# Two attention layers on one core: the first output group ahead of the value transposes, norm chunks between evictions

## The chip, the cores and the metric

The kernel runs on one core of one Trainium2 chip. The metric is the device time of one execution in microseconds (us). The engines of the core are named as the profile names them: PE (TensorE matmuls; PEld its weight loads), DVE (VectorE), ACT (ScalarE), POOL (GpSimd) and SP (SyncE, which here only issues DMA transfers). All data is fp32.

## The reference, cut to what matters

Two layers of the same shape run over x of (4, 32, 32, 768): a group norm over 32 groups of channels of each image, attention with 12 heads of 64 and decomposed relative position biases, an output projection, and a residual.

```python
x = x + _L0_conv_ref(_gn(x), L0_conv_Wqkv, L0_conv_Wproj, ...)
x = x + _L1_conv_ref(_gn(x), L1_conv_qkv_w, L1_conv_qkv_b, ...)

qkv = x @ Wqkv                                  # in each layer; layer 1 with a bias
rel_h = einsum('bhwc,hkc->bhwk', r_q, Rh)       # and rel_w likewise
scores = scale * einsum('bqc,bkc->bqk', q, k) + (rel_h[..., :, None] + rel_w[..., None, :])
out = einsum('bqk,bkc->bqc', softmax(scores), v)
return out @ Wproj + bproj
```

The norm's mean and variance are over a whole image's 1024 positions and 24 channels. So the norm of a layer's image needs the whole output of the layer before for that image.

## The kernel before, in words

**Images, pairs, units.** There are eight images in order (layer 0 images 0 to 3, then layer 1 images 0 to 3). An image is kept as six chunks of 128 channels by 1024 positions (`xn`). Heads go two at a time: 6 pairs an image, 48 in all. A pair has 8 units (n = 0 to 7), each the scores of 128 query positions for both heads against all 1024 keys. The loop at L521 goes over the 384 units; everything is issued by hand in the order of the code (`manual_schedule`, L497), so each engine works its own instructions in that order.

**One step of the loop** (L521 to L573) issues, in this order: the biases of the unit after next on POOL (L303); the scores of the next unit on PE (L315), with, for each of the two heads, a pass on DVE that adds the bias and finds the maximum (L324), and an exponential on ACT (L328); at n = 7 the transposes of the next pair's values on PE (`vt`, L252) with their copy out of PSUM on ACT (L253); the read-back of transposed softmax quarters (`pt<-td`, L363); at some steps a stage of the next image's norm; the softmax transposition of this unit on DVE (`turn`, L352), followed on every second step by a store to DRAM (`td<-tb`, L355); the reciprocal (L335, DVE) and the division (L338, POOL) of the next unit; then a share of a list of projection work. After n = 6 and n = 2 come the weighings of values with two quarters of the softmax (`av`, L378, copied out by DVE at L383).

**The list of projection work.** `todo` holds groups; `shares` says how many chunk matmuls of it each step takes: 6, 6, 0, 6, 12, 6, 0, 12 for n = 0 to 7. For each pair it holds six groups of the next pair's q, k and v (`pj`, L222, six chunks each; copied out by ACT at L232 or L234 and added by DVE at L235), then four groups of the output projection (`o`, L442, three chunks each, evicted by DVE). So at n = 7 the share of 12 is four output groups, whenever there are any.

**The output projection** of an image is done in parts: part 0 (heads 0 to 5) in pairs 3 to 5 of that image, evicted at L451 with output bias and residual, and stored as a partial sum to DRAM (`part<-res`); part 1 (heads 6 to 11) in pairs 0 to 2 of the next image, evicted at L454 with the partial sum loaded again (`res<-part`), followed in layer 0 by `bn_stats` for the next norm (L149). For the last image there is no next one: its parts 1 (chunks 3 and 4) and 2 (chunk 5) fill the last pair and the tail behind the loop (L574 to L586), where sums are kept on the chip (`sum`) from part 1 on.

**PSUM.** Scores have a pool of their own (L76). All other PE results (`pj`, `tp`, `vt`, `av`, `o`) share the two buffers of L77: what comes next on PE needs the buffer of what came two before, emptied by DVE or ACT.

**The norm of the next image.** At pair 3 four stages are issued (L556): at n = 1 per-channel statistics go to DRAM, at n = 3 they come back by group, at n = 6 `groups` computes the mean and inverse deviation (a square root on ACT at L187, for which ACT exchanges its function table and, for the next exponential, exchanges it back; then a reciprocal on DVE at L188 and a store), at n = 7 the result is spread to channels. At pair 4 the chunks are normed in place on DVE (`apply`, L197): chunk 0 at n = 2, chunk 1 at n = 6, chunks 2 to 5 at n = 7 after the first output group.

**Transfers.** SP issues nearly all DMAs in program order, and an issue that waits holds up those behind it. Lists (`early`, `later`, `behind`, `behind2`) put issues off to the next steps.

Of the kernel before, what the change touches and what calls it, by code (L numbers as in the profile page):

```python
# [54 lines left out]
def attention_blocks(ctx: ExitStack, tc: tile.TileContext, a: dict, out: bass.AP):  # L55
    nc = tc.nc
# [27 lines left out]
    NI = len(images)  # L84
# [45 lines left out]
    bo = []  # L130
# [32 lines left out]
    def norm(im):  # L163

        per = dram2.tile([C, 2], FP, tag="per", name=f"per_{im}")
        back = dram2.tile([C, 2], FP, tag="back", name=f"back_{im}")  # L170
        g = small.tile([NG, 2, GS, 2], FP, tag="g", bufs=1, name=f"g_{im}")
        st = small.tile([NG, 2, 6], FP, tag="gst", bufs=1, name=f"gst_{im}")
        mv = small.tile([NG, 3, 2], FP, tag="gmv", bufs=1, name=f"gmv_{im}")
        nrm = small.tile([P, NC, 2], FP, tag="nrm", bufs=2, name=f"nrm_{im}")

        def gather():
            nc.sync.dma_start(out=per.rearrange("(c p) s -> p c s", p=P), in_=mv_of[im])

        def by_group():
            nc.sync.dma_start(out=g[:, 0, :, :], in_=per.rearrange("(g k) s -> g k s", k=GS))  # L180

        def groups():
            for k in range(2):
                nc.vector.bn_stats(st[:, k, :], g[:, 0, :, k])
                nc.vector.bn_aggr(mv[:, k, :], st[:, k, :])
            nc.vector.tensor_scalar(mv[:, 2, 0:1], mv[:, 0, 1:2], mv[:, 1, 0:1], EPS, ALU.add, ALU.add)
            nc.scalar.activation(mv[:, 2, 1:2], mv[:, 2, 0:1], AF.Sqrt)  # L187
            nc.vector.reciprocal(mv[:, 2, 0:1], mv[:, 2, 1:2])  # L188
            for k, x in enumerate((mv[:, 0, 0:1], mv[:, 2, 0:1])):
                nc.vector.tensor_copy(g[:, 1, :, k], x.to_broadcast([NG, GS]))  # L190
            nc.sync.dma_start(out=back.rearrange("(g k) s -> g k s", k=GS), in_=g[:, 1, :, :])

        def spread():
            nc.sync.dma_start(out=nrm, in_=back.rearrange("(c p) s -> p c s", p=P))

        def apply(c):
            nc.vector.tensor_scalar(  # L197
                xn_of[im][c], xn_of[im][c], nrm[:, c, 0:1], nrm[:, c, 1:2], ALU.subtract, ALU.mult
            )

        return [gather, by_group, groups, spread], apply


    qkv_of, v_of, rel_of, t_of = {}, {}, {}, {}
# [186 lines left out]
    def cuts(im):  # L391
        return [0, NC // 2, NC] if im + 1 < NI else [0, NC // 2, NC - 1, NC]

    parts = [(im, p, o, i) for im in range(NI) for p in range(2) for o in range(NC) for i in range(2)]
    place = {part: at for at, part in enumerate(parts)}
    part_of, res_of, sum_of = {}, {}, {}
    fetched = [0, 0]
# [1 line left out]
    def fetch(upto):  # L399

        while fetched[0] <= min(upto + 2, len(parts) - 1):
            im, p, o, i = parts[fetched[0]]
            c0, c1 = cuts(im)[p : p + 2]
            if i == 0:
                w = wopool.tile([P, NC // 2, P], FP, tag="wo", name=f"wo_{im}_{p}_{o}")
                nc.sync.dma_start(
                    out=w[:, : c1 - c0, :],
                    in_=a[f"wo{images[im][0]}"][o][:, c0 * P : c1 * P].rearrange(
                        "p (c o) -> p c o", o=P
                    ),  # L410
                )
                for c in range(c0, c1):
                    wo_of[im, o, c] = w[:, c - c0, :]
            fetched[0] += 1
        while fetched[1] <= min(upto, len(parts) - 1):
            im, p, o, i = parts[fetched[1]]
            l, b = images[im]
            if (p, o, i) == (0, 0, 0):
                part_of[im] = dram2.tile([C, S], FP, tag="part", name=f"part_{im}")
            res = iopool.tile([P, HALF], FP, tag="res", name=f"res_{im}_{p}_{o}_{i}")  # L420
            res_of[im, p, o, i] = res
            src = srcs[l][b] if p == 0 else part_of[im]
            nc.sync.dma_start(out=res, in_=src[o * P : (o + 1) * P, i * HALF : (i + 1) * HALF])
            fetched[1] += 1

    def fetch_last():
        im = NI - 1
        w = wpool.tile([P, NC, P], FP, tag="w", name="w_last")
        src = a[f"wo{images[im][0]}"].rearrange("o p (c k) -> c p o k", c=NC)
        nc.sync.dma_start(out=w, in_=src[NC - 1])  # L430
        for o in range(NC):
            wo_of[im, o, NC - 1] = w[:, o, :]
            sum_of[o] = xpool.tile([P, S], FP, tag="xn", name=f"sum_{o}")

    def project_out(im, p, o, i):
        l, b = images[im]
        rows = slice(o * P, (o + 1) * P)
        cols = slice(i * HALF, (i + 1) * HALF)
        c0, c1 = cuts(im)[p : p + 2]
        t = ps_m.tile([P, S], FP, tag="m", name=f"o_{im}_{p}_{o}_{i}")[:, :HALF]  # L440
        for c in range(c0, c1):
            nc.tensor.matmul(  # L442
                t, lhsT=wo_of[im, o, c], rhs=attn_of[im * NP + c][:, cols],
                start=(c == c0), stop=(c == c1 - 1),
            )
            if c < c1 - 1:
                yield True
        at_end = im + 1 == NI and p > 0
        res = sum_of[o][:, cols] if at_end else res_of[im, p, o, i]
        if p == 0:  # L450
            nc.vector.scalar_tensor_tensor(res, t, bo[l][:, o : o + 1], res, ALU.add, ALU.add)  # L451
        else:
            add = res_of[im, p, o, i] if p == 1 else res
            nc.vector.tensor_tensor(res, t, add, ALU.add)  # L454
        if p == 1 and l + 1 < LAYERS:
            stats(im + B, o, i, res)
        dst = part_of[im] if p == 0 else dsts[l][b]
        if at_end:
            if p == 2:
                nc.sync.dma_start(out=dst[rows, cols], in_=res)  # L460
        else:
            early.append(lambda: nc.sync.dma_start(out=dst[rows, cols], in_=res))
        if i == 1 and p < 2:
            (early if im + 1 == NI else later).append(lambda: fetch(place[im, p, o, i] + 4))
        yield True


# [5 lines left out]
    def run(todo):  # L473
        while todo:
            todo.pop(0)()
# [21 lines left out]
    with tc.manual_schedule(engines=ENGINES):  # L497
# [4 lines left out]
        for stage in stages:  # L502
            stage()
        for c in range(NC):
            apply(c)
        todo = prepare(0)
# [14 lines left out]
        for at, (g, n) in enumerate(units):  # L521
            im, pair = divmod(g, NP)
            end = im + 1 == NI
            if n == 0:
                shares = [6, 6, 0, 6, 12, 6, 0, 12]
                ins = (todo if at == 0 else []) + (prepare(g + 1) if g + 1 < NPAIR else [])
                if pair < 3:
                    if at == 0:
                        shares = [12, 6, 0, 6, 12, 6, 0, 0]
                    todo = ins + (put_out(im - 1, 1, range(4 * pair, 4 * pair + 4)) if im else [])  # L530
                elif pair < NP - 1:
                    todo = ins + put_out(im, 0, range(4 * pair - 12, 4 * pair - 8))
                    if pair == 3 and not end:
                        stages, apply = norm(im + 1)
                else:
                    todo = ins + put_out(im, 0, range(8, 12))
                    if end:
                        fetch_last()
                        todo += put_out(im, 1, range(12)) + put_out(im, 2, range(0, 12, 2))
                        shares = [0, 6, 6, 4, 2, 2, 0, 8]  # L540
            if pair < 3 and not end and n % 4 == 0 and 2 * pair + n // 4 < AHEAD:
                load_x(im + 1, 2 * pair + n // 4)
            if pair < 3 and im + 1 < B and n in (1, 3, 5, 6):
# [5 lines left out]
                biases(*units[at + 2])  # L549
            if at + 1 < len(units):  # L550
                scores(*units[at + 1])
            if late and n == NT - 1 or at == 1:
# [81 lines left out]
```

## Time and profile before

| | |
|---|---|
| time, median of 3 runs | 3668.21 us (3663.29 to 3672.43) |
| profiled execution | span 3666.7 us, mean granted PE clock 0.993 |
| busy share PE / DVE / POOL / ACT | 96% / 66% / 63% / 36% |
| L222 `pj`, L315 `s`, L378 `av`, L442 `o` on PE, busy | 1533.7, 751.1, 687.8, 524.0 us |
| DMA | 1090.58 MB, mean 297 GB/s |
| `td<-tb`, `pt<-td`: 1024 KB each, x384 each | median 5.8 and 7.7 us to landing |

The page's first part gives the busy time of each engine; the span less PE's busy time is what PE stood idle. The waits view says for which instruction an engine waited, in total and how often. The timeline gives start, length, engine, line, operation, `out<-in` and, in brackets, how long the engine had been idle and what ended it; matmuls of one kind are merged into one line (fp32 matmuls count twice, so a group of three chunks of L442 is six). The view of windows gives busy times and the granted PE clock of chosen stretches.

### The profile page before, as it was taken

The numbers are of one execution on the slowest core, as the hardware profiler recorded it, in microseconds if no ns is written. First come the engines' busy times: TensorE is split into PE (matmuls) and PEld (weight loads), VectorE is DVE, ScalarE is ACT, GpSimd is POOL, SyncE is SP. The second block draws the span as 40 slices with busy tenths as digits, with TensorE's granted clock in tenths as the row PEclk, the third lists the DMA queues.
The fourth block names the chain that finished last, engine by engine and source line by source line (L and its number), as shares of the span: only waits on it lengthen the run. The fifth ranks groups of instructions, "written<-read, shape, count | busy, mean of one in ns | idle before, by whom it ended". The sixth has DMA issues, their size and how long they took to land.

```text
span 3666.7 us, 51253 instructions
## 1 busy us (share of the span) xinstructions
PE 3530.5 (96%) x19200; PEld 1739.5 (47%) x19200; DVE 2401.9 (66%) x3533; ACT 1309.5 (36%) x1992; POOL 2298.0 (63%) x1548
## 2 busy tenths in 40 slices
PE   6999999999999999999999999999999999999998
PEld 3554444444445444444445444444445444444443
DVE  4676667766676676666666666666666667666664
ACT  2343333333333333333333333333333333333331
POOL 3776666665666666666666666666656666666662
PEclk9999999999999999999999999999999999999999
DMA  4998898888988888888898888988889888888877
GB/s 142 321 313 299 290 324 311 305 292 284 327 313 304 278 314 312 310 297 284 296 317 307 283 305 305 317 303 289 303 285 320 288 294 315 300 303 286 306 277 277
DMA packets 632345, 1090.58 MB, mean 297 GB/s; under 512 B 248096, under 2 KB 310304, under 8 KB 582944
## 3 DMA queue, kind: packets, MB, share of 16 engines
q1 hardware_dynamic: 581408, 1036.97, 80.8%
q10 hardware_dynamic: 50688, 50.34, 3.9%
q8 instruction: 151, 2.47, 0.3%
q14 instruction: 98, 0.80, 0.1%
HBM read 583.74 MB, written 503.41 MB: 296 GB/s over the span
## 4 chain that ended last, share of the span: by engine, by line
PE 88%; ACT 4%; DVE 3%; DMA 2%; issue 2%; SPq 0%; POOL 0%; DVEq 0%; ACTq 0%; POOLq 0%
PE pj L222 40%; PE s L315 18%; PE av L378 17%; PE o L442 10%; ACT sc L328 3%; PE tp L267 3%; DVE xn L197 1%; ACT v L253 1%; DVE sc L324 1%; DVE res L451 0%; DMA pt<-td 0%; DMA xs<-in_x 0%; DVE tb L352 0%; DMA w<-in_wqkv 0%; DMA part<-res 0%
## 5 line engine op out<-in xcount | busy, mean ns | idle before, releaser
L338 POOL TENSOR_SCALAR sc<-sc,sm 128x1024 f32<-128x1024 f32 x768 | 852.2, 1122 | 1265.8 <-DVE sm L335 1233.5
L222 PE MATMUL pj<-xn,w 64*128 64x512 f32 x6912 | 1533.7, 590 | 26.9 <-DVE xn L197 25.9
L303 POOL TENSOR_TENSOR sc<-rel 128x1024 f32<-128x1024 f32 x768 | 1457.0, 1918 | 42.1 <-DMA rel<-tdr 42.1
L328 ACT ACTIVATE sc<-sc,sm 128x1024 f32<-128x1024 f32 x768 | 879.1, 1145 | 1482.2 <-DVE sm L324 1482.1
L324 DVE CUSTOM_DVE_ANT_0 sc<-s,sc 128x1024 f32<-128x1024 f32 x768 | 909.6, 1222 | 290.4 <-PE s L315 273.4
L222 PEld LDWEIGHTS pj<-xn,w 64*128 64x128 f32 x6912 | 676.8, 187 | 837.4 <-issue 807.9
L352 DVE STREAM_TRANSPOSE tb<-sc 128x1024 f32<-128x1024 f32 x768 | 909.9, 1222 | 8.7 <-DMA td<-tb 7.9
L315 PE MATMUL s<-k,q 64*128 64x512 f32 x3072 | 751.1, 598 | 8.5 <-DVE sm L324 8.3
L378 PE MATMUL av<-pt,v 128*64 128x256 f32 x6144 | 687.8, 381 | 3.4 <-DVE res L451 3.1
L442 PE MATMUL o<-attn,wo 128*128 128x512 f32 x1128 | 524.0, 614 | 93.3 <-ACT v L253 44.2
L378 PEld LDWEIGHTS av<-pt,v 128*64 128x64 f32 x6144 | 433.9, 137 | 286.8 <-issue 31.8
L315 PEld LDWEIGHTS s<-k,q 64*128 64x128 f32 x3072 | 289.3, 187 | 342.9 <-issue 321.7
L442 PEld LDWEIGHTS o<-attn,wo 128*128 128x128 f32 x1128 | 211.4, 195 | 370.6 <-issue 229.8
L235 DVE TENSOR_TENSOR v<-pj,v 128x512 f32<-128x512 f32 x96 | 108.1, 1126 | 294.3 <-ACT v L234 142.6
L272 ACT COPY t<-tp 128x1024 f32<-128x1024 f32 x96 | 97.1, 1012 | 216.5 <-PE tp L267 216.1
L383 DVE COPY attn<-av 128x512 f32<-128x512 f32 (+1 forms) x97 | 66.2, 683 | 165.0 <-PE av L378 165.0
L451 DVE SCALAR_TENSOR_TENSOR res<-o,bo,res 128x512 f32<-128x512 f32 x96 | 70.7, 744 | 129.4 <-PE o L442 127.6
L328 ACT ACTIVATION_READ_ACCUMULATOR sc<-sc,sm 128x1 f32 x768 | 143.4, 187 | 0.0
L235 DVE TENSOR_TENSOR q<-pj,q 128x512 f32<-128x512 f32 x96 | 66.4, 692 | 108.7 <-ACT q L232 57.0
L235 DVE TENSOR_TENSOR k<-pj,k 128x512 f32<-128x512 f32 x96 | 66.4, 692 | 105.2 <-ACT k L232 53.5
L454 DVE TENSOR_TENSOR res<-o,res 128x512 f32<-128x512 f32 x84 | 57.6, 686 | 96.8 <-PE o L442 96.8
L267 PEld LDWEIGHTS tp<-tab,q 64*128 64x128 f32 x1536 | 99.0, 187 | 40.7 <-issue 40.3
(38 smaller groups left out, 816.2 us busy)
## 6 DMA issues: line engine op xcount, KB each, us to landing
td<-tb SPq DMA_DIRECT2D x384, 1024.0 KB, 5.8
pt<-td SPq DMA_DIRECT2D x384, 1024.0 KB, 7.7
w<-in_wqkv SPq DMA_DIRECT2D x144, 384.0 KB, 6.8
tdr<-t ACTq DMA_DIRECT2D x96, 512.0 KB, 6.4
rel<-tdr SPq DMA_DIRECT2D x768, 32.0 KB, 2.2
part<-res SPq DMA_DIRECT2D x96, 256.0 KB, 3.3
res<-part SPq DMA_DIRECT2D x96, 256.0 KB, 8.3
wo<-in_wo SPq DMA_DIRECT2D x90, 192.0 KB, 8.1
```

Source lines behind the costliest of these rows:

```text
L222: nc.tensor.matmul(t[:, a, :], lhsT=w[rows, c, :], rhs=xn[c][rows, cols], start=(c == 0), stop=(c == NC - 1),)
L235: nc.vector.tensor_tensor(to, t[1], to, ALU.add)
L267: nc.tensor.matmul(ps[:, h, j, :], lhsT=q[rows, at * P : (at + 1) * P], rhs=tabs[l][rows, :], start=True, stop=True,)
L272: nc.scalar.copy(t, ps.rearrange("p h j r -> p j h r"))
L303: nc.gpsimd.tensor_tensor(sc, rel[:, h, 0, n, :].unsqueeze(2).to_broadcast([P, HW, HW]), rel[:, h, 1, n, :].unsqueeze(1).to_broadcast([P, ...
L315: nc.tensor.matmul(ps[h][:, cols], lhsT=q[rows, n * P : (n + 1) * P], rhs=k[rows, cols], start=True, stop=True,)
L324: nc.vector.tensor_tensor_reduce(out=sc, in0=ps[h], in1=sc, scale=-scale, scalar=BIG, op0=ALU.add, op1=ALU.min, accum_out=st[:, 0, h : h + 1],
L328: nc.scalar.activation(sc, sc, AF.Exp, bias=st[:, 0, h : h + 1], scale=-1.0, accum_out=st[:, 1, h : h + 1],)
L338: nc.gpsimd.tensor_scalar(sc, sc, st[:, 2, h : h + 1], 1.0, ALU.mult, ALU.mult)
L352: nc.vector.transpose(tb[:, :, j, :], sc_of[g, n, h])
L378: nc.tensor.matmul(av[rows, at * 2 * P : (at + 1) * 2 * P], lhsT=v_of[g][:, k, rows], rhs=pt_of[g, quarter, h][:, :, k, :], start=(k == 0) ...
L442: nc.tensor.matmul(t, lhsT=wo_of[im, o, c], rhs=attn_of[im * NP + c][:, cols], start=(c == c0), stop=(c == c1 - 1),)
```

## The change

The change has four parts.

*Order within a step.* The value transposes move behind the read-back and the norm's stages, and at n = 7 a quarter of the share is taken ahead of them and of the softmax transposition. With a share of 12 that is one whole output group with its eviction. It is meant to let group 1's eviction go ahead of the transpositions on DVE, and to put another group between the value transposes and the reuse of their buffer.

*Norm.* The stages go to n = 1, 2, 4, 5 and 7: the square root is issued at n = 4, and what needs it (reciprocal, spreading within groups, store) at n = 5 as a stage of its own, `inverses`. Chunks 0, 1 and 2 are normed at n = 2, 4 and 6 of pair 4, and at n = 7 chunks 3 and 4 after the second output group and chunk 5 after the third.

*Last image.* Part 0 puts its result straight into `sum` on the chip, without the store to DRAM; part 1 adds to it without the load. The output weights of chunks 3 to 5 are loaded by three loads of 384 KB (`w_last`) in place of one such load and six small ones.

*Last pair and tail.* Its shares become 0, 6, 6, 6, 6, 2, 0, 4, and the last read-back is issued from ACT's queue rather than SP's.

```diff
@@ norm
             nc.scalar.activation(mv[:, 2, 1:2], mv[:, 2, 0:1], AF.Sqrt)
+
+        def inverses():
             nc.vector.reciprocal(mv[:, 2, 0:1], mv[:, 2, 1:2])
...
-        return [gather, by_group, groups, spread], apply
+        return {1: gather, 2: by_group, 4: groups, 5: inverses, 7: spread}, apply
@@ output projection
-    parts = [(im, p, o, i) for im in range(NI) for p in range(2) for o in range(NC) for i in range(2)]
+    parts = [
+        (im, p, o, i) for im in range(NI) for p in range(2 if im + 1 < NI else 1)
+        for o in range(NC) for i in range(2)
+    ]
...
+        for c in range(NC // 2, NC):
+            w = wpool.tile([P, NC, P], FP, tag="w", name=f"w_last_{c}")
+            nc.sync.dma_start(out=w, in_=src[c])
+            for o in range(NC):
+                wo_of[NI - 1, o, c] = w[:, o, :]
...
+        to = sum_of[o][:, cols] if end else res_of[im, p, o, i]
         if p == 0:
-            nc.vector.scalar_tensor_tensor(res, t, bo[l][:, o : o + 1], res, ALU.add, ALU.add)
+            res = res_of[im, p, o, i]
+            nc.vector.scalar_tensor_tensor(to, t, bo[l][:, o : o + 1], res, ALU.add, ALU.add)
         else:
-            add = res_of[im, p, o, i] if p == 1 else res
-            nc.vector.tensor_tensor(res, t, add, ALU.add)
+            nc.vector.tensor_tensor(to, t, to, ALU.add)
@@ the loop
-                        shares = [0, 6, 6, 4, 2, 2, 0, 8]
+                        shares = [0, 6, 6, 6, 6, 2, 0, 4]
...
+            run(behind)
+            behind, behind2 = behind2, behind
+            if pair == 3 and n in stages and not end:
+                stages[n]()
+            if pair == 4 and n in (2, 4, 6) and not end:
+                apply(n // 2 - 1)
+            share = shares[n]
+            if n == NT - 1:
+                take(todo, share // 4)
+                share -= share // 4
             if late and n == NT - 1 or at == 1:
                 late.pop(0)()
-            run(behind)
-            behind, behind2 = behind2, behind
-            if pair == 3 and n in (1, 3, 6, 7) and not end:
-                stages[(1, 3, 6, 7).index(n)]()
-            if pair == 4 and n in (2, 6) and not end:
-                apply(n // 4)
             turn(g, n)
             if at + 1 < len(units):
                 divide(*units[at + 1])
-            share = shares[n]
             if pair == 4 and n == 7 and not end:
-                take(todo, 3)
-                share -= 3
-                for c in range(2, NC):
-                    apply(c)
+                for chunks in ((3, 4), (5,)):
+                    take(todo, 3)
+                    share -= 3
+                    for c in chunks:
+                        apply(c)
             take(todo, share)
...
-        run(behind)
+        for read in behind:
+            read(nc.scalar)
         run(early)
         run(later)
-        for read in behind2:
-            read(nc.scalar)
```

More of the change, by code (lines that the diff above doesn't have):

```diff
@@ L417, in fetch @@
             l, b = images[im]
-            if (p, o, i) == (0, 0, 0):
+            if (p, o, i) == (0, 0, 0) and im + 1 < NI:
                 part_of[im] = dram2.tile([C, S], FP, tag="part", name=f"part_{im}")
@@ L426, in fetch_last @@
     def fetch_last():
[L427 to L433, printed above, removed]
+        l = images[NI - 1][0]
+        src = a[f"wo{l}"].rearrange("o p (c k) -> c p o k", c=NC)
+        for c in range(NC // 2, NC):
[3 more added lines that the diff above has]
+                wo_of[NI - 1, o, c] = w[:, o, :]
     def project_out(im, p, o, i):
         l, b = images[im]
+        end = im + 1 == NI
         rows = slice(o * P, (o + 1) * P)
@@ L447, in project_out @@
                 yield True
-        at_end = im + 1 == NI and p > 0
-        res = sum_of[o][:, cols] if at_end else res_of[im, p, o, i]
+        if end and (p, i) == (0, 0):
+            sum_of[o] = xpool.tile([P, S], FP, tag="xn", name=f"sum_{o}")
+        to = sum_of[o][:, cols] if end else res_of[im, p, o, i]
         if p == 0:
-            nc.vector.scalar_tensor_tensor(res, t, bo[l][:, o : o + 1], res, ALU.add, ALU.add)
-        else:
-            add = res_of[im, p, o, i] if p == 1 else res
-            nc.vector.tensor_tensor(res, t, add, ALU.add)
+            res = res_of[im, p, o, i]
+            nc.vector.scalar_tensor_tensor(to, t, bo[l][:, o : o + 1], res, ALU.add, ALU.add)
+        else:
+            nc.vector.tensor_tensor(to, t, to, ALU.add)
         if p == 1 and l + 1 < LAYERS:
[L456 to L464, printed above, removed]
+            stats(im + B, o, i, to)
+        dst = (part_of[im] if p == 0 and not end else dsts[l][b])[rows, cols]
+        if not end:
+            early.append(lambda: nc.sync.dma_start(out=dst, in_=to))
+        elif p == 2:
+            nc.sync.dma_start(out=dst, in_=to)
+        if i == 1 and (im, p, o, i) in place:
+            (early if end else later).append(lambda: fetch(place[im, p, o, i] + 4))
         yield True
@@ L501, in attention_blocks @@
         stages, apply = norm(0)
-        for stage in stages:
-            stage()
+        for n in sorted(stages):
+            stages[n]()
         for c in range(NC):
@@ L551, in attention_blocks @@
                 scores(*units[at + 1])
+            run(behind)
+            behind, behind2 = behind2, behind
+            if pair == 3 and n in stages and not end:
+                stages[n]()
+            if pair == 4 and n in (2, 4, 6) and not end:
[4 more added lines that the diff above has]
+                share -= share // 4
             if late and n == NT - 1 or at == 1:
                 late.pop(0)()
-            run(behind)
-            behind, behind2 = behind2, behind
-            if pair == 3 and n in (1, 3, 6, 7) and not end:
-                stages[(1, 3, 6, 7).index(n)]()
-            if pair == 4 and n in (2, 6) and not end:
-                apply(n // 4)
             turn(g, n)
```

## The prediction

> **What bounds the kernel now.** I read part 1 of the page first: TensorE (PE) is busy 3530.5 of 3666.7 us, VectorE 66%, GpSimd 63%, ScalarE 36%, and the chain that ended last is PE for 88%. So time can come only from PE's 136 us of idleness, from its clock, and from the tail. Next, the waits of PE alone:
>
> ```profile
> PE o L442 <- ACT v L253: 44.2, 37, 1.5
> PE o L442 <- DVE res L451: 39.9, 14, 3.3
> PE pj L222 <- DVE xn L197: 25.9, 1, 25.9
> PE o L442 <- DVE sum L454: 9.1, 2, 8.1
> PE s L315 <- DVE sm L324: 8.3, 8, 2.3
> PE av L378 <- DVE res L451: 3.1, 1, 3.1
> ```
>
> (Columns: total us, times, longest.) Two thirds of the idleness stands before L442, the output projection; the 25.9 us are the start, which the change leaves alone. Third, the timeline of a last step (n = 7) of a pair, here pair 4 of the first image:
>
> ```profile
> 395.67 1.99 PE L315 MATMUL s<-k,q 64*128 64x512 f32 x8
> ...
> 397.59 1.09 PE L252 MATMUL vt<-ident,v 128*128 128x128 f32 x8
> 397.80 1.23 DVE L324 CUSTOM_DVE_ANT_0 sc<-s,sc 128x1024 f32<-128x1024 f32 x1 [1.29 <-PE s L315]
> ...
> 398.52 2.74 PE L442 MATMUL o<-attn,wo 128*128 128x512 f32 x6
> ...
> 400.09 2.37 DVE L352 STREAM_TRANSPOSE tb<-sc 128x1024 f32<-128x1024 f32 x2
> ...
> 400.27 1.13 ACT L328 ACTIVATE sc<-sc,sm 128x1024 f32<-128x1024 f32 x1
> ...
> 401.40 0.99 ACT L253 COPY v<-vt 128x1024 f32<-128x1024 f32 x1
> ...
> 402.43 0.73 DVE L451 SCALAR_TENSOR_TENSOR res<-o,bo,res 128x512 f32<-128x512 f32 x1
> 402.45 5.42 PE L442 MATMUL o<-attn,wo 128*128 128x512 f32 x12 [1.19 <-ACT v L253]
> ...
> 403.07 7.34 DVE L197 TENSOR_SCALAR xn<-xn,nrm 128x1024 f32<-128x1024 f32 x4
> ...
> 410.34 1.40 DVE L451 SCALAR_TENSOR_TENSOR res<-o,bo,res 128x512 f32<-128x512 f32 x2
> 411.13 2.84 PE L442 MATMUL o<-attn,wo 128*128 128x512 f32 x6 [3.27 <-DVE res L451]
> 413.90 1.99 PE L315 MATMUL s<-k,q 64*128 64x512 f32 x8
> ```
>
> The PSUM pool of L77 has two buffers. The value transposes (vt) take one, output group 1 the other; group 2 needs vt's, which ScalarE empties only after both exponentials (402.39), and the first eviction of an output group stands behind the two softmax transpositions. The four norm chunks then hold VectorE for 7.34 us, so group 4 waits again. Fourth, the granted clock, in the view of windows (stretch, us, PE, PEld, DVE, ACT, POOL busy, clock, DMA):
>
> ```profile
> 778.39:781.80 3.41, 3.41 (x5) 1.35 (x4) 0.40 (x1) 0.00 (x0) 3.41 (x3) 0.50 1.02 428
> 860.31:867.13 6.82, 5.72 (x8) 2.16 (x10) 1.90 (x4) 0.00 (x0) 0.00 (x0) 0.50 0.21 80
> ```
>
> Both follow a long wait (2.44 us before 777.11, 3.27 us before 861.40): the clock is halved for one or two stretches of 3.41 us. No wait of 1.19 us is followed by one.
>
> [...]
>
> **The change part by part.** Let t be time from the start of the scores at n = 7. One group is 2.57 us of PE (evictions at 3555.91, 3558.49, 3561.06 follow at that pace) and can be evicted 2.88 us after its start (in the next image group 2 starts at 554.10, its eviction at 556.98).
>
> *Loss removed per step.* From starts, since the displayed gap leaves out some pipeline tail: group 2 starts at 402.45, where 398.52 + 2.57 = 401.09 was possible: 1.36 us. At pair 3 the square root (L187) sits at n = 6, and the exponential's table load (1.28 us) falls into n = 7; there it is 326.83 - (321.67 + 2.57) = 2.59. At pair 4 group 4 starts at 411.13 and not at 402.45 + 5.14: 3.54 more. The waits show 37 + 14 cases: 37 x 1.36 + 7 x 2.59 + 7 x 3.54 = 50.3 + 18.1 + 24.8 = 93 us.
>
> *Clock removed.* Between 320 and 3556 us ten stretches are at half clock: after pair 3 at 327.8, 778.4, 1679.5, 2580.6 (four, PE busy throughout: 4 x 1.71 = 6.8), and after pair 4 at 860.3, 1761.4, 2662.5 (two each, 5.72 us of PE work at half: 3 x 2.86 = 8.6). Together 15 us.
>
> *What the new order leaves.* Group 1 goes first: PE 1.92 to 4.49, then vt to about 5.4. VectorE's two score passes end near 4.4, so group 1 is evicted from 4.80 to 5.53 (0.73), and group 2 can start at 5.58 where PE would like 5.42: a loss of 0.1 to 0.2 us, take 0.13. The vt buffer is emptied by ScalarE near 6.7; group 3 wants it at 8.1. The transpositions (2.37) run from 5.5, or 6.2 where statistics (0.69) come first, the reciprocal is done by 8.7, group 2 (ready at 8.4) is evicted by 9.4 at the latest, group 4 wants that buffer at 10.7. No wait. At pair 4: group 2 evicted by 9.2, chunks 3 and 4 (2 x 1.84) to 12.9, group 3 evicted to 13.6, chunk 5 to 15.4, group 4 evicted to 16.2. The next projection needs group 3's buffer at about 15, the sixth chunk about 4 us later: no wait. Chunks 1 and 2 at n = 4 and 6 (1.7 us each) lie under 12 and 7 us of PE work, and so does the root at n = 4, with the inverses at n = 5: its two table loads fall where PE has 5 to 10 us of projections queued, and VectorE no longer stands 2.04 us at the reciprocal. The transpositions end 1 to 2 us later against the scores, with td<-tb, read-back and weighing behind them; quarter 3 lands 8 to 10 us before its first matmul (start of av less landing of pt), so nothing. Body: 93 + 15 - 44 steps x 0.13 = 103 us.
>
> *The end (pair 5 of the last image, 3560.95 to the last eviction at 3663.72).*
>
> ```profile
> 3581.17 1.25 DVE L352 STREAM_TRANSPOSE tb<-sc 128x1024 f32<-128x1024 f32 x1 [2.76 <-DMA td<-tb]
> 3583.16 8.81 PE L378 MATMUL av<-pt,v 128*64 128x256 f32 x64 [3.07 <-DVE res L451]
> ...
> 3640.99 1.36 DVE L454 TENSOR_TENSOR sum<-o,res 128x512 f32<-128x512 f32 x2 [10.50 <-DMA res<-part]
> 3641.74 5.59 PE L442 MATMUL o<-attn,wo 128*128 128x512 f32 x8 [8.07 <-DVE sum L454]
> ```
>
> The partial sums of the last image now stay on the chip: 12 stores of 256 KB and 12 loads go, with six of the wo loads, against two more weight loads of 384 KB. So the last line's wait (8.07 us) goes with the load that it waited for, and so does its half clock (3638.8 to 3645.6, 3.84 us of PE work, 1.9 lost). The first: SyncE reached the read-back of the previous pair only at 3567.55 since it stood waiting for stores to free the residual buffers; without stores I put it near 3562.5. The writes issued at 3571.24 then don't queue behind it (it took 9.8 us instead of the median 5.8) and free the buffer near 3577, when the transposition wants it at 3578.4: av near 3580.4, not 3583.2, and without the half clock at 3584.1.
> From there I walked on by hand with the durations above. Groups of the second part are 1.72 us (four matmuls) and n = 3 and 4 have three each. VectorE evicts them only after scores and transpositions (4.8 us), so the third waits: about 2.4 and 2.2 us. Scores of the last unit near 3610.3, av of quarters 0 and 1 from 3612.4 to 3619.5. Now only two groups, not four, stand between this and quarter 2, whose transpositions end at 3613.4 and whose write and read-back (7 and 7 us under load) land near 3627: PE gets there at 3622.9 and waits 4 us. Then 3.5 (av) + 5.2 + 5.2 (groups), quarter 3 (landed near 3638) from 3640.9 to 3644.4, 0.5 for its copy, 5.2 for six groups, the last eviction near 3651. That is 12.8 us less than 3663.7; the new waits of over 2 us can bring half clocks, 1.7 each, and I take 2.8 for them. End: 10 us, between 2 and 15.
>
> *Sum:* 103 + 10 = 113; 3668.2 - 113 = 3555 us.
>
> **The rivals.**
> *The wait is replaced (0.15).* Two buffers remain, so group 2 now waits for group 1's own eviction by VectorE. If that comes late in each step (scores started late by the bookkeeping of n = 6), a loss of 0.7 instead of 0.13 stays: 44 x 0.57 = 25 us given back, 3580. For: margin is only 0.3 us on VectorE (4.4 against 4.80). Against: the scores' passes started 2.12 us after PE's scores in every step that I looked at, idle before.
> *The transfers become the bound (0.07).* DMA is at 0.86 to 0.87 of its time in the body, and at 1.0 in most of a step; quarter 1 lands just 4 us before use. If the queue took half of the gain back, 3606. Against: quarter 1's chain lies between n = 3 and n = 6, which don't get shorter, and the mean rises by no more than 3%.
> *The end gains nothing or loses (0.08).* The 4 us become 8 or more with half clocks: 3566 to 3575.
> *Slower (0.02).* The softmax transpositions, later by 1 to 2 us, delay read-back so that PE waits at n = 2: with 3 us and a half clock (1.7) in each of 44 steps, 207 lost against 113 gained, 3762; in two thirds of them, 138 lost, 3693. Against: the 8 to 10 us above.
>
> **How the numbers follow.** The forecast has 0.68 and 3555. The body's terms are starts read from the trace, good to 0.1 us a step (4 us); the end is a walk, good to 8; medians of this kernel span 9 us. That makes 3543 low; high takes in the replaced wait, 3581. Within 0.3% (11 us) the change would have to lose 90% of the gain: 0.02, slower 0.02, faster 0.96.
>
> **What would show it.** After: L442 <- ACT v and L442 <- DVE res together under 12 us instead of 84; the period of a plain pair 72.7 us instead of 73.9; no half clock between 150 us and the last pair; no wait on res<-part; a new wait of av on pt<-td of 3 to 6 us at the end; L187's reciprocal no longer idle for 2.04 us. Wrong would be: 1 us and more left before group 2, waits of av at n = 2 or n = 6 in the body, or waits of the scores' evictions at n = 4 and 5 of pair 3 behind the table loads.

## The result and the profile after

The changed kernel takes 3558.21 us, median of 4 runs (3557.89 to 3558.56), the kernel before 3667.97 in the same comparison (3663.29 to 3672.43): a ratio of 0.970, interval 0.968 to 0.972, 110 us less. The forecast was 3555, the range 3543 to 3581.

The waits of PE in the changed kernel (engine, line, what it waited for, total us, times, longest; L449 is the former L442, L224 the former L222, L317 the former L315, L380 the former L378):

```profile
PE pj L224 <- DVE xn L199: 26.0, 1, 26.0
PE s L317 <- DVE sm L326: 7.3, 7, 2.0
PE o L449 <- DVE sum L462: 3.7, 2, 1.9
PE av L380 <- DMA pt<-td: 2.1, 2, 1.9
PE o L449 <- DVE attn L385: 0.5, 1, 0.5
```

The two lines of 44.2 and 39.9 us are gone, not merely shorter. What is left is the start (26.0), the scores of the first image and of the last pair (7.3), and new, small waits in the last pair. The page's first part agrees: PE is busy 3511.2 of 3556.0 us, 99%.

The timeline of the step shown of before, n = 7 of pair 4 of the first image:

```profile
394.95 1.99 PE L317 MATMUL s<-k,q 64*128 64x512 f32 x8
...
396.87 2.84 PE L449 MATMUL o<-attn,wo 128*128 128x512 f32 x6
397.08 1.23 DVE L326 CUSTOM_DVE_ANT_0 sc<-s,sc 128x1024 f32<-128x1024 f32 x1 [1.29 <-PE s L317]
...
399.55 1.04 PE L254 MATMUL vt<-ident,v 128*128 128x128 f32 x8
399.56 1.13 ACT L330 ACTIVATE sc<-sc,sm 128x1024 f32<-128x1024 f32 x1
399.75 0.75 DVE L460 SCALAR_TENSOR_TENSOR res<-o,bo,res 128x512 f32<-128x512 f32 x1 [0.29 <-PE o L449]
400.42 2.36 DVE L354 STREAM_TRANSPOSE tb<-sc 128x1024 f32<-128x1024 f32 x2
400.56 7.99 PE L449 MATMUL o<-attn,wo 128*128 128x512 f32 x18
...
400.69 0.99 ACT L255 COPY v<-vt 128x1024 f32<-128x1024 f32 x1
...
404.11 3.89 DVE L199 TENSOR_SCALAR xn<-xn,nrm 128x1024 f32<-128x1024 f32 x2
...
407.92 0.74 DVE L460 SCALAR_TENSOR_TENSOR res<-o,bo,res 128x512 f32<-128x512 f32 x1
408.48 1.99 PE L317 MATMUL s<-k,q 64*128 64x512 f32 x8
408.58 1.73 DVE L199 TENSOR_SCALAR xn<-xn,nrm 128x1024 f32<-128x1024 f32 x1
```

Three groups run in one piece from 400.56 (x18), with nothing in brackets: group 1 was evicted by 400.50. ACT's copy of the value transposes still stands behind the exponentials, until 401.68, but its buffer is wanted only by group 3, at about 403.1. The distance from these scores to the next is 13.53 us; before it was 18.23 (395.67 to 413.90). The third part of the change shows in the norm chunks between the evictions.

The granted clock, in the windows view (stretch, us, busy PE, PEld, DVE, ACT, POOL, clock, DMA share, GB/s):

```profile
62.30:69.10 6.80, 5.96 (x15) 2.23 (x16) 1.40 (x3) 1.72 (x4) 3.95 (x4) 0.50 0.99 352
140.00:3460.00 3320.00, 3319.15 (x18327) 1646.38 (x18324) 2276.25 (x3331) 1251.08 (x1904) 2199.42 (x1473) 1.00 0.88 311
```

PE is busy 3319.15 of 3320 us, at full clock throughout. The first line is a halved clock at the start, which the profiled run of before did not have and which has nothing to do with the change (below).

To compare kernels without such chance I cut each profiled span at two starts of scores: the first unit of pair 3 of the first image (before it there are no output groups) and unit 1 of the last pair. The stretch between is the body. A pair's period runs from the scores in its step n = 7 to those in the next pair's; a plain pair is one of pairs 0 to 2 of an image, without stages or chunks of the norm.

| kernel | start | body | last pair and tail | a plain pair |
|---|---|---|---|---|
| before | 255.1 | 3305.9 | 105.8 | 73.92 |
| changed | 258.4 | 3204.1 | 93.5 | 72.69 |

So the body gives 101.8 us and the end 12.3, and the start took 3.4 back in that one run.

### The profile page after: what moved, and what is told of

Read it like the earlier page. It is cut to its first block, busy times and chain, and to the rows that moved or that the text cites. A ratio compares the mean times of both kernels' runs of the same rounds, so it can differ in the third digit from the quotient of the medians.

```text
span 3556.0 us, 51176 instructions
## 1 busy us (share of the span) xinstructions
PE 3511.2 (99%) x19200; PEld 1733.6 (49%) x19200; DVE 2404.5 (68%) x3533; ACT 1309.4 (37%) x1992; POOL 2298.1 (65%) x1548
## 4 chain that ended last, share of the span: by engine, by line
PE 96%; DMA 2%; DVE 1%; POOL 1%; issue 0%; SPq 0%; ACT 0%; DVEq 0%; POOLq 0%
PE pj L224 41%; PE s L317 19%; PE av L380 19%; PE o L449 14%; PE tp L269 3%; PE vt L254 1%; DMA td<-tb 0%; DVE sc L326 0%; DVE tb L354 0%; POOL sc L305 0%; DMA w<-in_wqkv 0%; DMA xs<-in_x 0%; POOL sc L340 0%; SPq L295 0%; DMA pt<-td 0%
## 5 line engine op out<-in xcount | busy, mean ns | idle before, releaser
L224 PE MATMUL pj<-xn,w 64*128 64x512 f32 x6912 | 1537.1, 591 | 27.1 <-DVE xn L199 26.0
L224 PEld LDWEIGHTS pj<-xn,w 64*128 64x128 f32 x6912 | 674.8, 188 | 843.1 <-issue 813.3
L317 PE MATMUL s<-k,q 64*128 64x512 f32 x3072 | 752.1, 598 | 7.4 <-DVE sm L326 7.3
L380 PE MATMUL av<-pt,v 128*64 128x256 f32 x6144 | 685.7, 381 | 2.3 <-DMA pt<-td 2.1
L380 PEld LDWEIGHTS av<-pt,v 128*64 128x64 f32 x6144 | 433.0, 137 | 284.6 <-issue 29.6
L449 PE MATMUL o<-attn,wo 128*128 128x512 f32 x1080 | 487.5, 601 | 0.0
L317 PEld LDWEIGHTS s<-k,q 64*128 64x128 f32 x3072 | 288.3, 187 | 340.7 <-issue 321.4
L449 PEld LDWEIGHTS o<-attn,wo 128*128 128x128 f32 x1080 | 197.8, 190 | 258.1 <-issue 247.3
L460 DVE SCALAR_TENSOR_TENSOR res<-o,bo,res 128x512 f32<-128x512 f32 x84 | 62.9, 749 | 70.1 <-PE o L449 59.1
L269 PE MATMUL tp<-tab,q 64*128 64x128 f32 x1536 | 108.1, 278 | 0.0
```

The costliest lines, as they stand in the source:

```text
L224: nc.tensor.matmul(t[:, a, :], lhsT=w[rows, c, :], rhs=xn[c][rows, cols], start=(c == 0), stop=(c == NC - 1),)
L269: nc.tensor.matmul(ps[:, h, j, :], lhsT=q[rows, at * P : (at + 1) * P], rhs=tabs[l][rows, :], start=True, stop=True,)
L317: nc.tensor.matmul(ps[h][:, cols], lhsT=q[rows, n * P : (n + 1) * P], rhs=k[rows, cols], start=True, stop=True,)
L380: nc.tensor.matmul(av[rows, at * 2 * P : (at + 1) * 2 * P], lhsT=v_of[g][:, k, rows], rhs=pt_of[g, quarter, h][:, :, k, :], start=(k == 0) ...
L449: nc.tensor.matmul(t, lhsT=wo_of[im, o, c], rhs=attn_of[im * NP + c][:, cols], start=(c == c0), stop=(c == c1 - 1),)
```

## The experiments

All times are medians in us; "body" and "end" are the columns of the table above. Each kernel is the changed one with the edit shown, except where said. Kernels that are compared with the kernel before ran beside it on one chip.

**Which part carries the gain.** First the group taken ahead, removed:

```diff
-            if n == NT - 1:
-                take(todo, share // 4)
-                share -= share // 4
```

> The changed kernel without the group taken ahead: at n = 7 the value transposes, then the softmax transposition, then all four output groups; norm and last image as changed. My theory (group 2 waits for the buffer of the value transposes, which ACT empties only after two exponentials): 44 steps lose 1.36 - 0.19 = 1.17 us again, 51 us, so about 3609 us, and the wait of L442's line on ACT v is back near 44 x 1.2 = 52 us. Rival (the gain came from the norm's stages and chunks, and the order within the step matters little): 3558 to 3570.

Measured: 3611.9 (the kernel before, run beside it: 3668.7). Body 3258.4, 54.3 more than the changed kernel, 1.23 on average over 44 steps; a plain pair is back at 73.92. Its waits of PE:

```profile
PE o L449 <- ACT v L255: 53.7, 44, 2.3
```

That is 44 waits on ACT's copy again, one a step. The rival fell.

The new order alone, in the kernel before:

```diff
             run(behind)
             behind, behind2 = behind2, behind
...
+            share = shares[n]
+            if n == NT - 1:
+                take(todo, share // 4)
+                share -= share // 4
+            if late and n == NT - 1 or at == 1:
+                late.pop(0)()
             turn(g, n)
```

> The kernel before with the new order within the step alone; norm stages, chunks and last image as before. My theory: the order takes 37 x 1.17 us (43) and the first wait of pairs 3 and 4; the root at n = 6 then costs little, since group 1 no longer waits on ACT (exponentials 1.28 us later, the copy done at 8.0 us, wanted at 8.1): 0 to 0.5 us in 7 steps; the four chunks in a row still hold up group 3's eviction to 17.3 us where the next projection wants its buffer at 15: 2.3 us in 7 steps, 16, with some half clocks; the last image saves nothing. 3668 - 51 - 7 x 1.2 (root) - 7 x 1.2 (chunks) - half clocks 10 to 15 = about 3588, between 3578 and 3600. Rival (the parts only work together): 3630 and more.

Measured: 3583.4, body 3215.0, end 108.7. The order takes 90.9 of the body's 101.8 us and no half clock is left in the body. The norm chunks as before, in the changed kernel:

```diff
-            if pair == 4 and n in (2, 4, 6) and not end:
-                apply(n // 2 - 1)
+            if pair == 4 and n in (2, 6) and not end:
+                apply(n // 4)
...
-                for chunks in ((3, 4), (5,)):
-                    take(todo, 3)
-                    share -= 3
-                    for c in chunks:
-                        apply(c)
+                take(todo, 3)
+                share -= 3
+                for c in range(2, NC):
+                    apply(c)
```

> The changed kernel with the norm chunks as before: chunk 0 at n = 2, chunk 1 at n = 6, chunks 2 to 5 in a row (7.3 us) at n = 7 of pair 4, now behind group 2. My theory: group 3 is evicted at 17.3 us after the start of the scores where the next projection wants its buffer near 15: 2.3 us in each of 7 images, 16 us, plus half clocks of up to 2.9 us in some: 3574 to 3590. Rival (once group 1 goes first the chunks are hidden too): 3558 to 3562.

Measured: 3570.2, body 3215.0: 10.9 more, 1.55 in each of 7 images. From its timeline:

```profile
401.36 6.92 DVE L199 TENSOR_SCALAR xn<-xn,nrm 128x1024 f32<-128x1024 f32 x4
...
408.20 1.40 DVE L460 SCALAR_TENSOR_TENSOR res<-o,bo,res 128x512 f32<-128x512 f32 x2
409.00 5.42 PE L224 MATMUL pj<-xn,w 64*128 64x512 f32 x24 [1.28 <-DVE res L460]
```

The mechanism is the expected one: group 3's eviction waits behind four chunks, and the next pair's projection waits for its buffer. It costs less than I thought (1.55, not 2.3), and none of these waits was followed by a half clock. The norm's stages as before:

```diff
-        return {1: gather, 2: by_group, 4: groups, 5: inverses, 7: spread}, apply
+        return {1: gather, 3: by_group, 6: lambda: (groups(), inverses()), 7: spread}, apply
```

> The changed kernel with the norm's stages as before (n = 1, 3, 6, 7; root, reciprocal and store all at n = 6). The prediction counted 7 x 2.59 us at pair 3 and four half clocks as removed; this asks which part removes them. My theory: the order within the step does, since group 2 no longer waits on ACT behind the table load: 0 to 0.5 us in 7 steps, 3558 to 3562. Rival (the earlier root is needed): 7 x 1.23 us + half clocks, 9 to 20 us, 3567 to 3578.

Measured: 3558.8, body 3204.1, the same to 0.1 us. In its timeline the table load (1.28 us in the kernel before) is back at n = 7 of pair 3 and DVE stands 2.03 us at the reciprocal again, and neither costs time. The move of the square root is worth nothing beside the new order. The last image as before (partial sums through DRAM, weight loads, shares, last read-back), with the new order and the new norm, that is the hunks on `parts`, `fetch`, `fetch_last`, `project_out`, the last shares and the tail undone:

> The new order and the new norm, but the last image as before: partial sums through DRAM, old weight loads, old shares of the last pair, last read-back on SP. My theory: the end takes 12 us longer (wait of 8 us on the reloaded partial sum, the halved clock behind it, the wait of 3 us before av), 3568 to 3572. Rival (the end gained nothing): 3558.

Measured: 3570.2, body 3204.5, end 105.9, 12.5 more than the changed kernel. Its waits of PE:

```profile
PE o L444 <- DVE sum L456: 7.5, 2, 7.2
PE av L380 <- DVE res L453: 3.8, 1, 3.8
```

The parts add up: 12.0 (last image) + 11.9 (chunks) + 0.6 (root) over 3558.2 is 3582.7, and the order alone measured 3583.4.

**What in the order does it.** Taking group 1 ahead does two things: its matmuls come before the value transposes on PE, and its eviction before the softmax transposition on DVE. Each half alone. The eviction first, the value transposes still in front on PE:

```diff
+            if late and n == NT - 1 or at == 1:
+                late.pop(0)()
             if n == NT - 1:
                 take(todo, share // 4)
                 share -= share // 4
-            if late and n == NT - 1 or at == 1:
-                late.pop(0)()
```

> Half of the move: the first group goes ahead of the softmax transposition (so its eviction is early on DVE), but behind the value transposes on PE. My theory: group 2 again needs the buffer of the value transposes, so ACT's copy sets its start as before: 1.17 us in each of 44 steps, about 3609 us. Rival (what counted was the eviction's place on DVE, ahead of the transpositions): as the changed kernel, 3558.

Measured: 3611.5, body 3257.3, L449 <- ACT v 52.6 us in 44 waits: no gain to speak of over the kernel with no group ahead (body 3258.4). The matmuls first, the eviction behind the transposition (the eviction is put off in a list that runs after `divide`):

```diff
             if n == NT - 1:
+                hold[0] = True
                 take(todo, share // 4)
+                hold[0] = False
                 share -= share // 4
...
                 divide(*units[at + 1])
+            run(held)
```

> The other half: the first group's matmuls go ahead of the value transposes on PE, but its eviction stands behind the softmax transposition and the reciprocal on DVE. My theory: group 2 needs group 1's buffer, which is emptied at 7.7 us after the start of the scores and not at 5.5, a loss of about 2.3 us instead of 0.19 in each of 44 steps: 93 us, and waits of over 2 us can bring half clocks: 3650 to 3690, no better than the kernel before. Rival (what counted was the place on PE alone): 3558.

Measured: 3613.3, body 3257.3. Neither number held: no gain over the kernel with no group ahead, as my theory said, but a loss of 1.2 us a step and not of 2.3. Its timeline (n = 7 of the first pair of the second image) says why:

```profile
546.17 2.84 PE L449 MATMUL o<-attn,wo 128*128 128x512 f32 x6
...
548.85 1.04 PE L254 MATMUL vt<-ident,v 128*128 128x128 f32 x8
...
549.99 0.99 ACT L255 COPY v<-vt 128x1024 f32<-128x1024 f32 x1
...
551.01 0.67 DVE L464 TENSOR_TENSOR res<-o,res 128x512 f32<-128x512 f32 x1
551.03 7.99 PE L449 MATMUL o<-attn,wo 128*128 128x512 f32 x18 [1.15 <-ACT v L255]
```

Group 2 starts at 551.03, right behind ACT's copy (550.98) and before group 1's eviction ends (551.68). So it cannot be writing into group 1's buffer: it took that of the value transposes. The compiled programs say the same: in this step group 1 lies in PSUM banks 6 and 7, the value transposes in 4 and 5, and group 2 in 4 and 5; in the changed kernel groups 1 and 2 share banks and the transposes have the other two. My theory had the buffers alternate, and that step was wrong. I supposed next that a buffer goes to whoever comes after the first one given back in the order of the code, and put ACT's copy behind group 1's eviction in the code:

```diff
-        nc.scalar.copy(v_of[g], t)
+        held_v.append(lambda: nc.scalar.copy(v_of[g], t))
...
             run(held)
+            run(held_v)
```

> The changed kernel with group 1's matmuls first and its eviction behind the transposition and the reciprocal, and with ACT's copy of the value transposes written behind that eviction. In the earlier run with the matmuls alone first (3613 us), group 2 started at 551.03, while group 1's eviction ran until 551.68: it had taken the buffer of the value transposes, since that was given back first in the order of the code. Here group 1's is given back first; ACT's own order is the same. My theory: group 2 now waits for the late eviction, 0.7 us longer a step: 44 x 0.7 = 31, 3644 us, the wait at L449 put down to DVE instead of ACT, and some half clocks on top. Rival (the buffers alternate whatever the order of the code): as that run, 3613.

Measured: 3613.2, body 3257.5, and group 2 is in the transposes' banks again. That guess fell too. What the assignment goes by stays open. In ten of eleven compiled programs group 2 lies in the buffer that comes free first by the trace; in the kernel with the eviction alone first it lies in the transposes', though group 1's came free 0.3 to 0.6 us earlier.

The cost of a late eviction with group 2 in group 1's buffer can be read in the kernel before. In its last step of pair 3, in 7 of the 44 steps, the compiled program puts group 2 into group 1's banks:

```profile
321.67 2.74 PE L442 MATMUL o<-attn,wo 128*128 128x512 f32 x6
...
325.84 0.99 ACT L253 COPY v<-vt 128x1024 f32<-128x1024 f32 x1
...
326.05 0.73 DVE L451 SCALAR_TENSOR_TENSOR res<-o,bo,res 128x512 f32<-128x512 f32 x1
326.83 9.69 PE L442 MATMUL o<-attn,wo 128*128 128x512 f32 x18 [2.42 <-DVE res L451]
```

Group 2 waits there for an eviction that ends at 326.78, and the loss is the 2.59 us of the prediction, near the 2.3 expected of the late eviction. Here the other buffer would have been no better: ACT's copy, behind a table load (1.28 us from 322.26) and two exponentials, ends at 326.83.

What is shown: with group 2 in the transposes' buffer and the copy behind the exponentials each step loses 1.2 us, wherever group 1's matmuls or its eviction stand; with both ahead, group 2 gets group 1's buffer and the loss is gone.

If ACT's place in its queue is the cause, the copy could also go ahead of the exponentials. So the value transposes ahead of the scores:

```diff
+            if late and n == NT - 1:
+                late.pop(0)()
             if at + 1 < len(units):
                 scores(*units[at + 1])
...
-            if late and n == NT - 1 or at == 1:
+            if at == 1:
                 late.pop(0)()
```

> The changed kernel, with the value transposes at n = 7 ahead of the scores, so that ACT's copy of them stands ahead of the exponentials. If a queue place on ACT was the cause, nothing waits here either, and the 0.19 us that group 2 still loses goes too: 44 x 0.19 = 8 us less, 3550. [...] Together about 3564, between 3550 and 3573. Rival (the copy's place isn't the cause): waits of 1 us and more appear at L442's line, 3600.

Measured: 3559.7 (3557.5 to 3562.1), a plain pair 72.66 against 72.69, no wait at L449 in the body. Here group 2 lies in the transposes' banks and still does not wait, for the copy was done before the exponentials: in n = 7 of the first pair of the second image it ends at 544.02, the first exponential starts at 546.36. That is the cause shown from the other side. The body is 3201.6, 2.5 less than the changed kernel's; the last pair and tail are 3.7 longer, with two half clocks behind their waits, and a pair without output groups takes 64.80 us, not 63.77. The two small terms of my estimate, 8 us for and 14 against, are not separated by this run; together they come to 2.5 us for. The 14 us were my estimate, 44 x 0.33 us of idle time before weight loads; that PE loses 0.33 us by them was not shown, for it is the mean idle time before all weight loads of L442 in the kernel before (370.6 us before 1128).

**The last pair.** The changed kernel's own new waits are in its timeline:

```profile
3496.44 1.98 PE L449 MATMUL o<-attn,w_last 128*128 128x512 f32 x4 [1.86 <-DVE sum L462]
...
3505.82 1.98 PE L449 MATMUL o<-attn,w_last 128*128 128x512 f32 x4 [1.85 <-DVE sum L462]
...
3527.59 2.60 PE L380 MATMUL av<-pt,v 128*64 128x256 f32 x22 [1.94 <-DMA pt<-td]
```

They are those of the walk in the prediction: the third group of n = 3 and of n = 4 waits for an eviction behind the transposition, and quarter 2 comes too early. Two kernels tried to take them away, beside the changed kernel itself as the measure:

> The changed kernel itself, as the measure for the others on the same chip: 3558 us.

Measured: 3558.1 (3555.8 to 3560.5), body 3204.1, end 93.3, start 256.5. The old shares of the last pair:

```diff
-                        shares = [0, 6, 6, 6, 6, 2, 0, 4]
+                        shares = [0, 6, 6, 4, 2, 2, 0, 8]
```

> The changed kernel with the old shares of the last pair (0, 6, 6, 4, 2, 2, 0, 8). The new shares put three groups into n = 3 and n = 4, whose third waits 1.9 us each for an eviction behind the transpositions, and leave two groups ahead of quarter 2, which then waits 1.9 us. My theory: the sums kept on the chip are the end's whole gain, and the old shares fit it better: with two groups and one at n = 3 and 4 nothing waits, and four groups at n = 7 cover quarter 2's transfer: 4 us less, about 3554 us. Rival (the new shares carry part of the gain): 3560 to 3566.

Measured: 3552.1 (3548.8 to 3554.6), end 88.6, 4.7 less than the changed kernel run beside it. The new shares cost time; the rest of what was done for the last image carries the end's whole gain. That rest is the sums kept on the chip together with the three weight loads and the last read-back on ACT's queue, which no run separates. And the idea of the change taken into the last pair, with other shares:

```diff
-                        shares = [0, 6, 6, 6, 6, 2, 0, 4]
+                        shares = [0, 6, 6, 6, 4, 2, 0, 6]
...
-            if n == NT - 1:
-                take(todo, share // 4)
-                share -= share // 4
+            ahead = share // 4 if n == NT - 1 else 0
+            if end and pair == NP - 1:
+                ahead = {2: 3, 3: 2, 4: 2, 7: 2}.get(n, 0)
+            take(todo, ahead)
+            share -= ahead
```

> The changed kernel with the idea of the change carried into the last pair: one group with its eviction ahead of the softmax transposition also at n = 2, 3, 4 and 7, and shares 0, 6, 6, 6, 4, 2, 0, 6. The two waits of 1.9 us for the third group's buffer and most of the 1.9 us for quarter 2 go: 4 to 5 us less than the changed kernel, about 3553.5. Rival (each group put ahead delays the transpositions and with them the transfers, which set the end): 3558 or more.

Measured: 3550.2 (3550.1 to 3554.3), ratio to before 0.968 (0.967 to 0.969), end 87.1, 6.3 less. From its timeline, n = 3 of the last pair:

```profile
3489.27 5.42 PE L449 MATMUL o<-attn,w_last 128*128 128x512 f32 x12
...
3491.77 0.69 DVE L462 TENSOR_TENSOR sum<-o,sum 128x512 f32<-128x512 f32 x1
3492.38 2.36 DVE L354 STREAM_TRANSPOSE tb<-sc 128x1024 f32<-128x1024 f32 x2
```

The first group's eviction goes ahead of the transposition, and three groups run in one piece, so the 1.86 us at n = 3 went by the new order. At n = 4 this kernel has two groups and not three, and at n = 7 three and not two, so the other two waits may have gone by the shares alone, as they did with the old ones. Its median is the lowest of the study, 8 us below the changed one's (6 by the end alone), but its runs overlap with those of the old shares; by the end it is 1.5 us shorter than they are.

## Why the prediction was right, point by point

**Loss removed and left, per step.** Forecast 1.36 - 0.13 = 1.23 us for a plain step; measured 73.92 - 72.69 = 1.23 in pairs 0 to 2. In pair 5 the period is 72.75 and the gain 1.17, for there an eviction takes 0.75 us, not 0.69, and 0.19 us is left. Without the group ahead the same loss came back.

**Body.** Forecast 103 (93 of waits, 15 of half clock, 6 left); measured 101.8. The half clocks between 150 us and the last pair are gone, as forecast. The pair periods of the kernel before give their share: 76.86 against 75.17 us at pair 3, with a half clock and without, in four images, and 80.26 against 77.45 at pair 4 in three: 15.2 us where 15 was counted. The other 86.6 us are the waits, where 93 - 6 was counted.

**Where the chunks and the root stood.** The forecast's sum was right, but it let the parts of the change share it unsaid, and in its text the root's new place (n = 4) removes the table load (1.28 us) from n = 7. The runs show that the order alone took the loss away; the earlier root added nothing (3558.8). The DVE's wait at the reciprocal of 14.6 us in total (L188 in the kernel before, down to 0.3) was real and hidden. The walk through pair 4 held closely: group 2's eviction was put at 9.2 us after the scores and group 4's at 16.2; the trace has 404.19 - 394.95 = 9.24 and 410.98 - 394.95 = 16.03.

**The end.** Forecast 10, measured 12.3. The term that was mis-sized is "I take 2.8 for them", the half clocks behind the new waits. The waits were put at 2.4, 2.2 and 4 us and measured 1.86, 1.85 and 1.94 as displayed (2.12 and 2.11 from starts for the first two), and none of them was followed by a half clock in this run. The walk itself held: the read-back was issued 3.25 us after the first scores (I had 1.55; three weight loads, 4.23 us of issuing from 3457.29, and one more stand in front of it), av of the previous pair started at 19.33 us (I had 19.4), and the last eviction ended at 90.4 us (I had 90.1).

**The start.** Not in the forecast: 258.4 against 255.1 us in the profiled runs. The changed kernel run again had 256.5. Of the fourteen profiled runs eight have a halved stretch near 62 to 65 us and starts of 256.5 to 260.1, six have none and starts of 255.1 to 256.9. The half stretches lie differently in the two executions: counted from the span's start, they begin 0.15 us past a multiple of 3.413 us in the profiled run of before and 0.84 us past one in that of the changed kernel. That a wait is then hit or not by its position is my inference; the last section has figures for it.

**The rivals.** No wait took the place of the one removed: group 1's own eviction was in time, as the 0.3 us of margin (399.75, 0.29 us after DVE was free) had it. The transfers rose from 0.86 to 0.88 of the time in the body, and PE waits for none of them there. The nearest was quarter 1 of the softmax, which lands 1.2 us before its first matmul at the closest (1.4 in the kernel before; the prediction had 4). Later transpositions delayed nothing: quarter 3 still lands 7 us and more before its first matmul in the body's pairs with output groups. (In the kernel before it was 4.7 to 10.6 us, not the 8 to 10 of the prediction.)

**A step that was right by luck.** The prediction reckoned with two buffers that alternate. With both halves of the move in place that comes out right, and the numbers with it. With the matmuls alone first it does not, and the two expectations built on it or on its repair were wrong by 37 us or more and by 31. Nor did it hold in the kernel before: at pair 3 group 2 waited for group 1's late eviction, where the prediction saw the table load ahead of ACT's copy. The term of 2.59 us was read from starts, so it was right all the same; the two came free within 0.05 us of each other.

## What to carry to other kernels

Where two engines empty the same few PSUM buffers, ask which engine empties the buffer that the next group will get, and what stands in that engine's queue ahead of it: here two exponentials of 1.15 us in front of a copy cost PE 1.2 us a step, and moving either the group (with its eviction) or the copy ahead removed it. Which buffer the next group gets is to be read in the compiled program, not supposed to alternate. Putting one group and its eviction ahead of a long operation is worth trying wherever three groups share two buffers in one step; in the last pair it took away a wait of 1.86 us. Read the parts of a change apart: here one of them (the earlier root) brought nothing and one (the last shares) cost 5 us, which the sum of 110 us hid.

## What I had not expected of the hardware

Some waits well below the length of a stretch (3.41 us) were followed by a half clock. Outside the start, of some 210 waits of 1.14 to 1.5 us at L442 or L449 (37 to 44 in each of five kernels) none was followed by a half clock; of the 18 waits of 1.84 to 1.86 us in the last pairs of nine kernels three were; of those of 2.43 us at pair 3 in the kernel before four in seven; of those of 3.27 us at pair 4 three in seven, for two stretches each.

Which of equal waits were followed by one goes with where they fell. In each run all half stretches start on one grid of 3.413 us, to within 0.01 us (the eleven of the kernel before to within 0.001). I laid this grid over the fourteen traces from 150 us on and took the share of each stretch in which PE was idle. Of the stretches at full clock, those idle for 60% and more were all followed by a half one (19 of 19; 9 of 9 in the kernel before), those idle for less than half never (none of some 14,000; of 1005 there and 995 in the changed kernel), and those between in 6 of 22. The ends of matmuls are modelled, so these shares are no closer than that: at the start of the changed kernel a stretch idle for 49% was followed by a half one, at 62.28. The half stretch starts at the next line of the grid even while PE still waits (at 860.31, in a wait that ends at 861.40).

What follows for a single wait is my estimate from these figures, for the time after the start. A wait of 1.2 us is 35% of a stretch and stays below half of it wherever it falls. One of 1.86 us, 54%, takes up more than half only if nearly all of it lies in one stretch, and one of 2.43 us, 71%, if most of it does. So cutting a wait from 2.4 to 1.2 us was worth more than the 1.2 us: in the body of the kernel before, half clocks made up 15 of the 102 us.
